# One transformer-like stack on one core: the same operations in another order of issue

## The chip, the core and the metric

The kernel runs on one core of a Trainium2 chip. The time is the device time of one execution in microseconds, and a run's figure is the median of several executions. The core has a matrix engine (TensorE, PE in the profile, with PEld for its weight loads), a vector engine (VectorE, DVE), an activation engine (ScalarE, ACT), a general engine (GpSimd, POOL), and SyncE (SP), whose queue issues all DMAs of this kernel.

## What is computed

The input is x of 8 x 512 x 512 (8 images of 512 rows and 512 columns), in fp32. Four sublayers follow each other, each with a layer norm before and after and a residual sum:

```
x = x + ln(attn0(ln(x)))    # scores = X^T X, softmax over rows, context = weights X^T
x = x + ln(ffn0(ln(x)))     # x times the sum of 8 matrices (512 x 512), / sqrt(8), + bias
x = x + ln(attn1(ln(x)))    # RMS norm, 8 query heads in 2 groups of keys and values, Wo, residual
x = x + ln(ffn1(ln(x)))     # silu(x Wg * gs) * (x Wu * us), times Wd, * ds; inner width 1408
```

Here `ln` subtracts the mean and divides by the root of the variance.

## The kernel before

The 8 images are worked through one after the other in the source, each as four tiles of 128 rows x 512. The functions `stage_attn0`, `stage_ffn0`, `stage_attn1` and `stage_ffn1` do not issue instructions. They hand operations to a recorder (`rec.add`), each with its engine, the buffers that it reads and writes, and a closure that issues its instructions. This gives 6333 operations: 1220 for TensorE, 2174 for VectorE, 1238 for ScalarE, 952 for GpSimd and 749 DMAs. `rec.issue` then calls the closures in an order that is written out in the file: the text `STEPS` holds 6333 differences, and `order()` sums them into the numbers of operations:

```
n, found = -1, []
for step in STEPS.split():
    n += int(step)
    found.append(n)
```

Each engine gets its own instructions in that order and runs them in it, and waits on semaphores where one needs another engine's result. Buffers are handed out in the same order: an operation that opens a buffer takes the one that has been free longest among those of its kind (8 PSUM banks `f`, 15 tiles `row`, 33 tiles `fr` for weights and parts, 6 tiles `big`, 11 tiles `x`). So the order also decides which earlier work a new buffer waits for. In the given order the images overlap: while one image is in `stage_ffn1`, the next one is already in its attention.

The lines that the steps below name:

- L281 loads inputs and weights. L310 writes kept weight pieces to DRAM, and L321 fetches them back for the images 1 to 7. For these images most weights and rows are split in parts (L349, L357, L364 for weights; L380, L388, L397 for rows), and the products run on fp32r parts (L410 and L420, called one after the other as two groups of matmuls).
- A layer norm is L576 (statistics), L581 (aggregate), both on VectorE, L585 and L592 on GpSimd (`rstd`), and L600 on VectorE (normalize). L619 adds the result to x, on GpSimd, for the last image on VectorE.
- A softmax row is L633 (maximum, VectorE), L640 (exponential, ScalarE), L650 and L660 (VectorE).
- `stage_attn0`: L697 transposes on TensorE two tiles at a time, L725 copies the result on ScalarE. L753 computes a block of 128 rows of the symmetric score matrix; the part left of the diagonal comes by L751 as a transpose of earlier blocks, which L767 copied to the tiles `u` on ScalarE. L783 is the context product.
- `stage_ffn0`: L671 transposes, and for image 0 L828 (the mix) multiplies by the summed matrix, which L474 adds up on VectorE and GpSimd from 28 loaded tiles.
- `stage_attn1`: L1004 values (with the weight `wv`), L1043 queries, L1071 scores, L1102 transposes, L1114 copies them on ScalarE to the place where L1132 multiplies with the values, L1145 copies the result. L1177 is the last projection of image 0.
- `stage_ffn1`: L1251 and L1260 split the transposed rows, L1315 are the gate and up products, L1334 (silu, ScalarE), L1344 (product, VectorE), L1356 and L1363 (the two parts), L1373 the down product, L1399 its scale.

Of the kernel before, what the change touches and what calls it, by code (L numbers as in the profile page):

```python
# [1450 lines left out]
1 71 1 -71 75 1 -74 75 1 -6 1 15 -87 82 6 -5 -5 6 1 834 -846 -32 38 1 1 5 3 1 1 829 -902 905 1 4 1  # L1451
-7 19 -883 -10 2 45 1 5 -68 14 874 -867 -2 -35 9 -24 1 17 77 1 1 -50 2 2 872 1 -902 76 2 -47 875
-919 -6 98 833 -832 1 5 -4 5 1 -93 97 -24 850 -938 933 -824 -78 -3 82 -7 10 810 -812 3 1 -82 19
882 1 -8 1 -839 -71 -15 936 1 -824 1 812 12 -5 9 -928 13 2 73 -1 -14 -56 -15 2 926 -912 1 -34 51
-49 34 81 -1 2 -97 908 -876 893 -2 -887 -54 1 2 259 -207 61 -112 30 -15 257 1 -155 -5 1 1 -114 939
-888 -21 85 -100 926 -823 1 -73 -15 -30 15 32 216 -148 22 1 -19 1 -74 75 1 820 1 -686 -118 1 801
-22 -655 675 -923 928 -792 -11 -18 1 -93 122 -28 133 687 -680 -139 1 27 795 -794 -25 12 117 691 1
1 -824 28 1 -156 130 1 821 2 -1 -682 -6 -133 1 1 -6 68 -39 1 -23 67 -36 31 -55 66 747 -812 71 742
-775 1 -23 8 16 1 83 -107 1 796 -772 1 759 726 -1484 743 2 -660 675 -803 814 -749 -41 1 1 -25 1 57
-41 1 -16 17 795 -761 -50 1 55 742 15 -796 766 -781 65 78 -32 33 1379 -1399 -103 1 788 -694 -215  # L1460
160 1461 -1484 1 79 29 -2 1 2 -93 -15 1 92 1 -92 1 106 -12 -114 1 1 1 109 1 -79 -13 94 1 -112 1
151 -56 -67 14 56 -75 76 23 -10 48 -121 -38 122 668 -7 -671 11 -10 -97 -15 126 1 1 22 5 -19 -6 -1
8 -6 -95 102 1 1 -8 9 -8 1 -11 12 661 -654 1 1 1 1 -48 1 -60 86 -84 83 673 711 -725 15 -8 -760 131
630 8 -757 -10 115 656 10 6 -27 8 4 1 -785 128 636 9 13 1 -22 16 699 1 -693 -6 -16 23 686 -701 70
-69 -639 -5 734 -20 -78 -744 843 -43 -810 5 782 -720 -230 942 -1 5 -2 4 -666 1 713 1 1 1 -824 112
-138 868 1 -695 696 607 -1291 583 56 -22 -12 -709 769 1 638 -686 -656 31 -44 25 15 16 605 30 -646
1 6 1291 1 -1303 622 4 -610 -4 665 1 1 -50 1 21 -650 -24 8 21 -20 27 4 -15 -29 722 -677 -4 -25 707
-718 -14 733 -723 -9 733 -18 -701 703 -707 5 7 665 -676 14 691 -662 -12 2 -1 42 603 30 -692 1316
-1256 4 644 -711 712 -708 1316 -606 -681 633 -602 649 -720 75 647 -650 631 -622 -42 -37 74 -33 43
-85 674 29 19 -641 623 1 -694 36 -34 -1 60 4 -36 42 4 587 -659 69 -40 34 7 622 -619 562 -561 -47  # L1470
-26 692 -629 -34 4 675 -738 1 63 -4 34 645 1 1 -527 -212 102 -35 -4 -4 681 -636 -1 -35 4 -8 69 5
-69 65 -64 3 1 -3 74 -40 -40 10 60 -69 84 -14 3 7 619 -625 1206 -605 -53 1 -26 -587 75 63 -62 614
9 -628 -70 71 621 7 -623 -12 626 1 -690 692 9 -778 78 58 12 -7 -35 664 -107 -662 152 -48 -26 39
1216 -563 568 -1228 32 -1 522 -552 -5 1 15 31 -35 36 534 -565 -11 7 -11 5 -4 580 -534 509 26 -566
567 -571 651 -657 42 509 -550 1 67 -62 4 567 -566 58 -56 67 -10 -58 61 8 -7 -3 507 -506 13 -10 7
470 -538 72 571 -581 20 -323 1 309 -6 10 -45 -265 301 6 4 1 -10 475 -507 7 525 -488 -1 2 488 -537
12 4 522 -806 776 679 -567 -615 -4 12 38 -45 -4 81 -69 -11 507 2 -497 35 -33 1 56 465 -520 -12 66
-53 -12 67 438 -437 438 -505 73 -5 515 -527 -93 38 505 1 1 -439 539 1 -539 514 -509 -4 438 -497
573 -473 -99 1 1 31 30 536 -535 509 -508 1 -32 540 26 -40 -862 446 -40 -371 334 -8 25 477 40 -26
-540 33 98 2 -66 6 456 -522 43 477 1 -417 419 -529 50 1 489 -539 52 513 -25 -11 -476 -46 534 25 1  # L1480
2 -454 40 -45 23 40 -461 289 53 1 -53 528 12 -11 -528 1119 -554 -36 -381 392 2 -1 -471 -69 4 1 1
46 -5 6 -46 1 1 19 1 4 95 -94 -4 1 1 557 -554 1 29 16 -44 1 75 36 -95 2 -1 2 -16 1 -3 1 32 11 88
-105 84 -61 18 -45 -347 394 44 -94 1 4 -394 398 14 55 -44 -8 2 46 2 -44 484 545 -966 -494 12 519
-19 -86 4 14 4 4 14 4 -36 -23 2 61 14 4 43 62 -60 922 -964 -60 1 60 -25 50 -107 1 102 -484 520 -40
-3 47 -60 17 4 -63 2 75 -116 21 -436 532 -101 -8 -420 535 -85 44 25 36 1 -122 77 -59 43 2 -43 1 1
163 -151 -54 2 80 -22 -59 -9 7 23 2 -1 -2 63 1 52 28 -8 -14 -5 -94 81 -79 -14 84 2 -57 -16 17 24
-43 20 38 -37 432 -337 -55 97 -606 -11 1 537 14 4 4 3 -81 2 -3 62 -21 -39 56 365 -321 -18 12 331
-311 22 -616 539 22 43 -46 38 26 -628 919 -337 22 -87 392 4 -366 919 -918 -40 41 52 -594 502 -2 -1
71 4 -12 343 -301 1 -86 1 3 100 291 -1 2 -445 51 1 402 -361 1 55 282 -320 337 -319 311 -386 -705
1092 -8 4 -282 -47 -32 46 4 4 14 4 4 304 -9 8 2 -11 -372 -122 176 -583 591 -23 44 -20 321 -383 374  # L1490
-903 905 -913 600 59 -650 -8 592 -33 -25 387 -10 2 -904 -8 1 561 44 316 -919 569 -16 -547 605 -59
2 362 -345 1 1 345 -305 -605 607 1 1 349 -33 38 7 -401 395 -398 25 -23 45 -25 371 16 -56 41 -313
324 -6 1 -451 -4 56 43 -20 48 -49 23 364 -15 -322 9 -37 366 -15 5 5 6 -979 927 -14 61 -60 -922 2
621 360 -344 302 37 -1 11 -35 -7 1 -5 -18 -275 1 293 47 -1 -31 -29 -2 -4 2 66 -37 -6 -4 -293 1 1
292 10 -6 10 -33 -295 325 -6 10 -3 74 -39 -41 1 67 -58 75 -404 388 4 -62 2 -1 58 4 7 -10 -382 393
-103 96 -3 4 10 -72 1 27 -339 380 -393 387 -96 106 -33 24 6 -41 45 -397 388 -99 64 45 -432 821
-431 1 43 -32 -367 290 67 6 -362 352 5 40 -104 74 -14 15 31 -36 37 -105 63 6 63 -68 1 9 -4 5 434
-365 -68 1 56 4 1 -4 11 -460 461 3 -10 -4 15 -10 77 -220 214 -75 -58 432 -289 -7 5 -113 5 40 -4
-148 142 -62 73 -40 36 -6 1 -437 805 1 -394 102 -5 -2 3 -509 503 -103 406 743 -1133 -4 -6 40 1 1
-154 513 -406 48 -32 -4 -11 5 -4 405 1 -391 59 -533 567 -97 5 -4 -428 421 42 -41 1 72 1 6 -69 70  # L1500
-502 1 1 488 -487 503 -502 430 -1 -442 505 -504 499 1078 -1072 20 -14 -11 1 14 315 1 1 -389 390
-327 6 4 -515 512 4 1051 -1097 5 358 -351 -481 470 35 1 10 -34 -7 11 -10 358 -316 -1 -46 -470 1
831 2 -316 -32 -4 360 -371 1104 1 -1057 -78 31 363 -359 -537 548 -570 645 1 -75 -5 1 359 734 -1100
12 359 -280 9 992 -1078 -13 1 11 1080 -1032 26 1 1 270 -258 271 -5 -261 267 -283 278 -8 -268 -77
346 -268 1 -78 39 1 1038 -992 1 992 -726 5 -279 280 715 11 -997 1 -29 1020 -726 -263 1 -38 1 -14 2
-1 2 302 -300 1 46 -37 24 1006 -1029 24 -33 34 12 266 -311 -607 906 -1 -218 -46 1004 1 -1030 3 -2
303 -300 1 1 31 -45 1 45 -31 1 31 1 263 2 -249 -62 1 14 52 1 -21 16 255 -270 -32 53 256 -276 1 2 1
289 -291 27 -14 40 244 -232 -51 1 -12 16 1 1 -17 1 1 16 246 -245 -14 1 14 67 -39 14 230 -289 262
-244 15 -32 267 -5 1 5 -4 5 1 -17 1 1 10 22 -14 1 1 -244 225 15 -250 269 -9 -5 6 -25 56 -36 1 2 34
1 -267 224 -226 -26 958 -644 -55 76 1 -334 38 -26 301 22 -334 1 334 1 -334 47 -803 1067 1 -276 -14  # L1510
313 -298 299 -326 24 12 215 -2 78 -104 34 -208 -14 3 290 -327 302 -22 -25 -6 -252 946 -942 302 1 1
23 1 -48 25 24 -73 1 1 73 -50 49 613 -684 73 -26 1 1 -259 -48 37 244 -22 23 -271 1 271 1 1 23 1 23
1 -47 -298 13 259 1 1 -272 -1 3 318 -319 320 1 -49 50 -49 50 -289 263 -275 13 308 1 -321 273 -284
81 231 -26 1 653 -627 -314 334 -278 15 -2 220 70 1 -25 -45 1 -266 45 193 -179 180 -261 44 -45 263
1 1 1 95 -267 -51 63 184 72 -71 -279 -1 256 1 -236 2 325 8 -7 8 -24 27 -26 1 -77 94 -15 -291 -43
358 -102 -177 -80 927 -593 2 -303 318 -317 318 -330 334 1 -334 298 32 7 -38 -226 2 -85 57 255 -311
-3 326 1 -326 45 266 3 35 1 -38 -289 1 36 -26 -20 33 304 -336 -2 -1 58 -40 297 1 44 10 -9 1 -59 1
1 1 11 1 -247 -27 299 -273 249 21 1 1 10 -7 9 -340 -1 8 -6 19 -11 24 -28 350 2 5 -28 -4 9 2 -319 1
330 -351 8 1 35 -1 298 -329 -1 2 -3 23 307 -306 11 1 306 -330 312 8 -316 304 1 12 -10 2 21 -309
-12 22 -34 335 -1 -10 -322 -1 325 20 -7 -14 11 -300 1 -21 -2 313 57 -40 9 36 1 -5 11 -381 382 -6  # L1520
10 -56 41 1 5 6 -373 13 364 -373 359 11 4 -62 59 -48 -14 13 -11 2 62 -11 2 -1 -352 363 -62 15 -291
# [211 lines left out]
```

## Time and profile before

| | |
|---|---|
| median of 3 runs | 1440.98 us (1439.24 to 1441.07) |
| the profiled execution | 1439.27 us |
| its span, first to last instruction | 1437.8 us |
| granted TensorE clock, mean | 0.993 of full |
| HBM read, written | 168.05 MB, 27.26 MB |

The span is what the profile's times are counted in. Busy times are the union of an engine's instructions; a matmul's end is modelled, so a busy TensorE can still hold small stalls. A line of the timeline has the start, the length, the engine, the line of the kernel, the operation, the tiles and their shapes, the count, and in brackets the engine's idle time before it with the instruction that ended it.

### The profile page before, as it was taken

The page shows a single profiled execution, that of the slowest core. Times are in us where ns is not written, and L with a number is a line of the kernel's source. Part 1 is how long each engine was busy: PE and PEld are TensorE (multiplying, and loading weights), DVE is VectorE, ACT ScalarE, POOL GpSimd, SP SyncE. Part 2 cuts the span into 40 slices and gives each one's busy share as a digit, 9 for nine tenths or more (in the row PEclk, how much of TensorE's full clock was granted, in tenths as well). Part 3 has the DMA queues.
Part 4 walks back from the last instruction along what each step waited for, and adds up shares of the span by engine and source line. Part 5 has one row for each costly group of instructions (what it writes and reads, how often), then busy time and mean ns, then how long its engine had stood idle before and what let it go on. Part 6 is the DMA issues. An engine that isn't in the chain of part 4 may idle for free.

```text
span 1437.8 us, 25008 instructions
## 1 busy us (share of the span) xinstructions
PE 1389.1 (97%) x8926; PEld 976.0 (68%) x8926; DVE 1030.0 (72%) x2175; ACT 734.4 (51%) x1638; POOL 764.5 (53%) x962
## 2 busy tenths in 40 slices
PE   6899989999999999999999999999999999999995
PEld 3445568656886668856687567865688666876784
DVE  7998886888638887388764886568874778638933
ACT  2337565682347723576335744457334583357621
POOL 6874437236851378415764177631887117850443
PEclk9999999999999999999999999999999999999998
DMA  7361287645422165124443162413624304532351
GB/s 266 130 208 57 83 264 269 201 137 191 150 92 89 38 235 176 52 74 138 165 152 107 56 210 92 169 36 134 213 81 147 118 23 165 190 121 83 117 206 47
DMA packets 123350, 197.06 MB, mean 137 GB/s; under 512 B 12496, under 2 KB 32976, under 8 KB 123216
## 3 DMA queue, kind: packets, MB, share of 16 engines
q1 hardware_dynamic: 123216, 195.36, 40.0%
q8 instruction: 73, 1.20, 0.3%
q14 instruction: 61, 0.50, 0.1%
HBM read 168.05 MB, written 27.26 MB: 136 GB/s over the span
## 4 chain that ended last, share of the span: by engine, by line
PE 76%; DVE 11%; POOL 7%; issue 3%; ACT 2%; DMA 0%; SPq 0%; POOLq 0%; DVEq 0%; ACTq 0%
PE f L1315 19%; PE f L1373 10%; PE f L410 9%; PE f L1071 8%; PE f L1132 7%; PE f L1102 5%; PE f L420 5%; PE f L753 4%; PE f L783 3%; DVE row L600 3%; POOL rstd L592 2%; POOL x L619 2%; DVE st L576 2%; PE f L1004 2%; PE f L697 1%
## 5 line engine op out<-in xcount | busy, mean ns | idle before, releaser
L1315 PE MATMUL f<-xs,fr 128*128 128x512 f32 (+1 forms) x1472 | 341.2, 383 | 1.8 <-ACT xs L1251 1.2
L1315 PEld LDWEIGHTS f<-xs,fr 128*128 128x128 f32 x1472 | 267.3, 188 | 58.2 <-issue 1.7
L633 DVE TENSOR_REDUCE s<-f 128x1 f32<-128x512 f32 x288 | 188.2, 683 | 68.2 <-PE f L1071 48.3
L640 ACT ACTIVATE row<-f,s 128x512 f32<-128x512 f32 x288 | 197.4, 696 | 57.8 <-DVE s L633 48.6
L619 POOL TENSOR_TENSOR x<-x,row 128x512 f32<-128x512 f32 x120 | 157.7, 1318 | 118.3 <-DVE row L600 96.3
L585 POOL TENSOR_SCALAR ve<-mv 128x1 f32<-128x1 f32 x224 | 60.0, 271 | 278.3 <-DVE mv L581 234.2
L1373 PE MATMUL f<-fr,hl 128*128 128x512 f32 x704 | 187.6, 396 | 0.4 <-POOL hl L1363 0.2
L410 PE MATMUL f<-fr,fr 128*128 128x512 f32 x728 | 185.0, 397 | 1.3 <-ACT big L1145 0.5
L1363 POOL TENSOR_TENSOR hl<-row,hl 128x512 fp32r<-128x512 f32 (+1 forms) x92 | 116.3, 1270 | 123.9 <-ACT hl L1356 121.8
L1114 ACT COPY big<-f 128x512 f32<-128x512 f32 x256 | 138.1, 594 | 55.8 <-PE f L1102 54.1
L1344 DVE SCALAR_TENSOR_TENSOR row<-f,us,row 128x512 f32<-128x512 f32 (+1 forms) x92 | 65.8, 720 | 136.4 <-PE f L1315 67.1
L410 PEld LDWEIGHTS f<-fr,fr 128*128 128x128 f32 x728 | 133.7, 188 | 35.4 <-ACT big L1114 1.8
L1373 PEld LDWEIGHTS f<-fr,hl 128*128 128x128 f32 x704 | 128.9, 188 | 38.8 <-issue 10.2
L660 DVE TENSOR_SCALAR row<-row,s 128x512 f32<-128x512 f32 x288 | 150.6, 549 | 1.7
L592 POOL TENSOR_TENSOR rstd<-ve,mhalf 128x1 f32<-128x1 f32 x224 | 137.6, 618 | 14.1
L1071 PE MATMUL f<-row,big 64*128 64x512 f32 x512 | 134.1, 617 | 0.0
L1356 ACT CAST hl<-row 128x512 fp32r<-128x512 f32 (+1 forms) x92 | 54.9, 603 | 144.7 <-DVE row L1344 87.7
L1132 PE MATMUL f<-big,row 128*64 128x256 f32 x1024 | 124.0, 385 | 3.5 <-ACT big L1114 3.4
L1334 ACT ACTIVATE row<-f,gs 128x512 f32<-128x512 f32 (+1 forms) x92 | 60.3, 667 | 123.4 <-PE f L1315 123.2
L388 POOL TENSOR_TENSOR fr<-big,fr 128x512 fp32r<-128x512 f32 x56 | 74.9, 1346 | 87.0 <-ACT fr L380 87.0
L397 POOL TENSOR_TENSOR fr<-fr,fr 128x512 fp32r<-128x512 f32 x84 | 110.7, 1325 | 9.7 <-ACT fr L380 3.9
L783 PE MATMUL f<-big,big 128*128 128x512 f32 x256 | 114.1, 596 | 0.0
(102 smaller groups left out, 2086.9 us busy)
## 6 DMA issues: line engine op xcount, KB each, us to landing
fr<-kept_g SPq DMA_DIRECT2D x81, 256.0 KB, 4.3
fr<-kept_u SPq DMA_DIRECT2D x81, 256.0 KB, 5.2
fr<-kept_d SPq DMA_DIRECT2D x81, 256.0 KB, 5.3
x<-in_x SPq DMA_DIRECT2D x32, 256.0 KB, 2.7
out<-x SPq DMA_DIRECT2D x32, 256.0 KB, 2.1
row<-in_factors SPq DMA_DIRECT2D x28, 256.0 KB, 4.9
row<-in_gate_t SPq DMA_DIRECT2D x11, 256.0 KB, 5.3
row<-in_up_t SPq DMA_DIRECT2D x11, 256.0 KB, 3.9
```

Source lines behind the costliest of these rows:

```text
L410: nc.tensor.matmul(both[0].t[:, :], lhs(q, k), rhs(q, k), start=(k == 0 and q == 0), stop=(k == KT - 1 and q == 1),)
L592: lambda: nc.gpsimd.tensor_tensor(rstd.t[:, :], ve.t[:, :], mhalf, ALU.pow),
L619: lambda: on.tensor_tensor(ap(xt), ap(xt), y.t[:, :], ALU.add),
L633: lambda: nc.vector.tensor_reduce(nmax.t[:, :], sc.t[:, :], AX.X, ALU.max, negate=True),
L640: lambda: nc.scalar.activation(e.t[:, :], sc.t[:, :], AF.Exp, bias=nmax.t[:, :], accum_out=tot.t[:, :]),
L660: nc.vector.tensor_scalar(e.t[:, :], e.t[:, :], rtot.t[:, :], None, ALU.mult)
L783: nc.tensor.matmul(po.t[:, :], xnT.t[:, j, ts(t, P)], wT.t[:, j, :], start=(j == 0), stop=(j == KT - 1),)
L1071: nc.tensor.matmul(scs[g].t[:, :], qT.t[gp, i, ts(s, P)], kT.t[gp, :], start=True, stop=True,)
L1114: copy(columns_of(aT)[:, :, lo : lo + DH], halves(pts[hf]))
L1132: nc.tensor.matmul(po.t[gp, : 2 * P], v.t[:, t * P + g * DH : t * P + (g + 1) * DH], columns_of(aT)[:, g * NT + t, :], start=(t == 0), sto ...
L1315: nc.tensor.matmul(bank.t[:, cut], w.t[:, ts(kt, P)], d.t[:, kt, cut], start=(n == 0), stop=(n == KT * len(xs) - 1),)
L1373: nc.tensor.matmul(pos[t].t[:, :], part.t[:, ts(t, P)], wd.t[:, :], start=(first and n == 0), stop=(last and n == len(parts) - 1),)
```

## The change

The text `STEPS` is replaced by another one of the same length. It comes from the same search for an order as the old one, which ran three times as long. The first line of each:

```
-1 71 1 -71 75 1 -74 75 1 -6 1 15 -87 82 6 -5 -5 6 1 834 -846 -32 38 1 1 5 3 1 1 829 -902 905 1 4 1
+4 86 1 -90 71 -70 71 19 1 -19 1 -72 74 8 -7 1 195 1 -195 6 8 -18 5 841 -835 1 1 -84 16 902 1 -895
```

All 6333 operations are the same, with the same instructions, tiles and buffers of each kind. What differs is their sequence on the engines and which buffer of its kind each gets. Nearly half of it is local: on TensorE 492 of 1220 operations keep their place in the engine's sequence, and half move by one place at most, nine in ten by five at most; on VectorE the figures are 441 of 2174, two and seven; on SyncE 61 of 749, five and seventeen. TensorE's sequence at the start, with the lines of the operations (image 0 up to the first L783, a comma between operations):

```
before: L697 (tiles 0, 1), L753, L751+L753, L751+L753, L751+L753, L697 (tiles 2, 3), L697, L697, ...
after:  L697 (tiles 0, 1), L753, L697 (tiles 2, 3), L751+L753, L751+L753, L751+L753, L697, L697, ...
```

ScalarE's sequence around the second and third score block of image 1 (L767 copies to `u`, L640 exponentials, L349 and L725 as above):

```
before: L725, L640, L767, L349, L640, L349, L767, L725, L349, L767, L640
after:  L640, L725, L767, L725, L767, L349, L349, L349, L349, L640, L767
```

VectorE's sequence at the end, from the first L1399 (the number is the tile of 128 rows):

```
before: L1399 1, L1399 0, L576 1, L576 0, L581 1, L1399 2, L1399 3, L576 2, L600 1, L581 2, L581 0,
        L619 1, L576 3, L600 2, L600 0, L581 3, L619 2, L619 0, L600 3, L619 3
after:  L1399 1, L1399 2, L576 1, L576 2, L1399 0, L1399 3, L581 1, L576 3, L581 2, L576 0, L600 1,
        L581 0, L581 3, L619 1, L600 2, L600 0, L619 2, L619 0, L600 3, L619 3
```

## The prediction

> **What bounds the kernel now.** I read the page's first part, then busy time by stretches, then TensorE's waits stretch by stretch, and last the timelines around the waits. The page first:
>
> ```profile
> PE 1389.1 (97%) x8926; PEld 976.0 (68%) x8926; DVE 1030.0 (72%) x2175; ACT 734.4 (51%) x1638; POOL 764.5 (53%) x962
> ```
>
> TensorE is busy 1389.1 of 1437.8 us, so a new order of the same work can take at most the other 48.7 us, and whatever stall hides inside "busy". Where the 48.7 us lie, by stretches (start:end, length, busy PE, PEld, DVE, ACT, POOL, granted clock, DMA):
>
> ```profile
> 0.00:36.00 36.00, 24.98 (x137) 14.12 (x138) 25.76 (x43) 9.98 (x21) 23.53 (x37) 0.95 0.79 266
> 36.00:96.00 60.00, 52.41 (x221) 26.59 (x220) 54.99 (x110) 19.05 (x47) 47.01 (x64) 1.00 0.49 161
> 96.00:180.00 84.00, 83.75 (x608) 47.86 (x606) 71.88 (x175) 53.10 (x126) 42.39 (x60) 1.00 0.29 90
> 180.00:216.00 36.00, 30.85 (x205) 25.10 (x204) 29.52 (x52) 23.47 (x50) 12.61 (x17) 0.95 0.82 265
> 216.00:1296.00 1080.00, 1071.85 (x6845) 767.02 (x6843) 762.00 (x1612) 563.86 (x1247) 592.83 (x728) 1.00 0.39 134
> 1296.00:1424.00 128.00, 125.26 (x917) 95.32 (x916) 79.18 (x175) 64.96 (x147) 42.38 (x53) 1.00 0.32 113
> 1424.00:1437.80 13.80, 0.00 (x0) 0.00 (x0) 6.64 (x15) 0.00 (x0) 3.80 (x7) 0.56 0.22 82
> ```
>
> Subtract busy PE from each length: 11.0 idle at the start, 7.6 in 36:96, 0.3, 5.2 in 180:216, only 8.2 in the 1080 us that follow, 2.7 before the end, 13.8 after the last matmul. Half of the idle time lies in image 0, where VectorE is the busiest engine (54.99 of 60), and the tail. The body is nearly full, and a better order has little to win there.
>
> **The change, part by part.** The counts of instructions stay the same on every engine, so the sum holds only waits that move. I decoded both orders into operations and went through the places above.
>
> Start. The first transposes (L697) need the normalized tiles 0 and 1. Before, VectorE writes them in the order 1, 0, 2, 3; after, 3, 0, 1, 2, so TensorE starts on the third and not on the second.
>
> ```profile
> 8.71 0.55 DVE L600 TENSOR_SCALAR big<-x,mv,rstd 128x512 f32<-128x512 f32 x1 [0.46 <-POOL rstd L592]
> 8.31 1.11 PE L697 MATMUL f<-ident,big 64*128 64x64 f32 x16 [8.31 <-DVE big L600]
> ```
>
> The third ends at 8.71 + 0.55 = 9.26, so the first matmul moves from 8.31 to about 9.3: +1.0. Against it, the second pair of transposes (0.55 us) moves into the wait for L767's copy ahead of the second score block (0.57 us), but the softmax rows after it end last anyway. Some of the delay is regained at the rows, as VectorE takes its statistics of image 1 earlier: I take +0.6, bounds 0 and +1.0.
>
> Image 0, 36:96. ScalarE runs its queue in order, and the copy to `u` (L767) that the third score block of image 1 needs stands behind a softmax exponential (L640) that waits 6.83 us for VectorE:
>
> ```profile
> 47.87 0.33 PE L751 MATMUL f<-ident,u 128*128 128x128 f32 x1 [3.14 <-ACT u L767]
> 55.65 0.65 PE L671 MATMUL f<-ident,row 128*128 128x128 f32 x4 [1.85 <-DVE row L600]
> ...
> 46.26 0.69 ACT L640 ACTIVATE row<-f,s 128x512 f32<-128x512 f32 x1 [6.83 <-DVE s L633]
> 46.94 0.62 ACT L349 ACTIVATE fr<-row 128x512 fp32r<-128x512 f32 x1
> 47.45 0.36 ACT L767 COPY u<-f 128x256 f32<-128x256 f32 x1
> ```
>
> After, this copy stands ahead of that exponential, and the weight split L349 at 46.94 is done at the very start. The copy can then run when its block ends (38.44 + 2.75 = 41.2), and the 3.14 us wait goes. What is late next is VectorE. The next L671 needs a row that VectorE normalizes with 34.9 us of its work queued ahead (32.7 before), the one after it 36.9 (37.6), and the last softmax row before the fourth mix 47.7 (47.2), by medians of its operations. So its queue is no shorter where TensorE meets it again. Between 0 and -3.1; I take -1.4, since VectorE has 60 - 55 = 5 us of idle time here that an earlier score block lets it use, and less than half of that is near those rows.
>
> Image 0, 180:216. Waits of 2.1, 1.3 and 1.3 us lie on the chain from the last projection (ends 180.6) through two layer norms to the gate products (193.7). VectorE's work ahead of the last normalization is 160.1 us in both orders; one statistics operation moves up by 2.5 us, and one load of `wv` moves behind the last projection. It is issued from 180.7 and takes a median 5.0 us, which lands at 185.7, ahead of its matmuls at 186.5: hidden, and up to +1.0 if the queue is longer. I take 0, bounds -1.5 and +1.0.
>
> The body, 216:1296. Who keeps TensorE waiting there:
>
> ```profile
> PE f L1132 <- ACT big L1114: 2.7, 8, 0.7
> PE f L697 <- DVE row L600: 2.3, 7, 0.5
> ```
>
> L1132 needs ScalarE's copies (L1114) of the transposes L1102. I added up the TensorE work between the last such transposes and each L1132, with the trace's start-to-start times: less than 1.5 us stands there in 14 of the 64 cases before, in 9 of 64 after. In that proportion 2.7 becomes 1.7: -1.0. Bounds: -8.2 (all idle gone) and +6.8 (the second rival).
>
> Changes of array shape. A run of matmuls that follows one of another kind costs a little more; it counts as busy and not as idle:
>
> ```profile
> 1056.56 2.10 PE L410 MATMUL f<-fr,fr 128*128 128x512 f32 x8
> 1058.49 1.09 PE L420 MATMUL f<-fr,fr 128*128 128x512 f32 x4
> ...
> 764.98 3.64 PE f L410 x16
> ```
>
> Eight alone take 1058.49 - 1056.56 = 1.93 us to the next start; sixteen in a row take 3.64, so eight take 1.82: about 0.1 us for a change. The old order has 371 changes, the new 365: -0.6. The page "Trainium Kernel Development and Optimization", Performance Expectations, calls matmul busy time a bad measure of closeness to the limit and LDWEIGHTS busy a good one; here they are 97% and 68%. By that rule more could be won than the 48.7 us, but at 0.1 us a change the 371 hold only 37 us, and the new order removes six.
>
> The tail. From the last matmul's end (1423.2) VectorE works through four layer norms, with two waits for GpSimd:
>
> ```profile
> 1427.37 1.17 DVE L600 TENSOR_SCALAR row<-row,mv,rstd 128x512 f32<-128x512 f32 x2 [0.33 <-POOL rstd L592]
> 1430.26 0.55 DVE L600 TENSOR_SCALAR row<-row,mv,rstd 128x512 f32<-128x512 f32 x1 [0.46 <-POOL rstd L592]
> ```
>
> After, all four statistics and aggregates stand ahead of the second normalization, so GpSimd has the last `rstd` early. The last sum still ends with the last matmul, and the first is free five matmuls before it in both orders. Both waits go: -0.33 - 0.46 = -0.8; at worst 0.
>
> Sum: +0.6 - 1.4 + 0 - 1.0 - 0.6 - 0.8 = -3.2 us. The profiled execution took 1439.27 us (span 1437.8), 1.7 below the median of the runs, 1440.98. So 1436.1 on its basis and 1437.8 as the median.
>
> **The clock.** The granted clock is 0.95 in 0:36 and in 180:216, where TensorE idles in pieces, and 1.00 elsewhere up to the end. One score block at reduced clock, starting at 26.41, lasts 5.22 us; the same block lasts 3.63 at 301.85. One such stretch more or less is 1.6 us, and lies inside the range. "TensorE: Matmul & The Clock Gate", Part 1, says that the window which decides this runs free of the program, so that the same kernel meets it differently from run to run. By that rule the change could gain or lose such a stretch by chance.
>
> **Rivals.** No change that can be told (within 0.2%, 2.9 us, about what a measurement of this kernel can tell from no change). The wait in 36:96 goes, but VectorE, 92% busy there, ends at the same time; then the sum is +0.6 - 0.6 - 0.8 and the body as it was: -0.8, 1440.2. For it: VectorE's queue ahead of its rows is equal or longer. Against it: the ScalarE row above shows a pure matter of order.
>
> Slower, by ScalarE's queue in attention. The 256 copies L1114 each have an operation directly ahead of them; it is one from another stage (neither a copy, an exponential nor L1145) 19 times before and 30 after. ScalarE's rows for such operations are near 0.62 us. If all 11 more are met by TensorE, 11 x 0.62 = +6.8; with the start at +1.0, the tail and the shape changes as above and no gain in 36:96, that is 1440.98 + 6.8 + 1.0 - 1.4 = 1447.4. It decides from about 5 of the 11 on (5 x 0.62 = 3.1). Against it: ScalarE is busy only 564 of 1080 us there, and most L1132 still have over 1.5 us of cover.
>
> Faster by much: all 3.1 in 36:96, half of the body's 8.2, 1.5 in 180:216, tail and changes as in the sum, nothing lost at the start: -3.1 - 4.1 - 1.5 - 0.8 - 0.6 = -10.1, 1430.9.
>
> That the table does not do what it says is not open: same operations, another sequence.
>
> **How the numbers follow.** The forecast, with its own range of 1434 to 1440, 0.36; the much faster case 0.10; no change 0.32; the slower one 0.22. Some of the forecast's part lies above -2.9 us, and a little of the even one below it, so: faster by over 0.2% 0.43, within 0.35, slower 0.22. The range leaves out half of the very fast case and less than half of the slow one: 1432 to 1446.
>
> **What would show it.** In the new profile: the first L697 at about 9.3 us; no wait of L751 for L767 near 45 us; fewer waits of L1132 for L1114 than 8 in the body; no wait for `rstd` among the last four L600; busy PE lower by half a microsecond or so. It is wrong if TensorE's idle time in the body rises above 10 us, if a wait for a DMA appears before L1004 or L1315, or if the first score block of a later image comes later than before although image 0 ended sooner.

## The result: slower by 0.4%, and the profile after

The new order takes 1445.88 us in the median of five executions (1443.36 to 1448.16), the old one 1440.87 beside it: ratio 1.0040, 95% interval 1.0029 to 1.0051. I had forecast 1437.8, and the result lies inside my range of 1432 to 1446, almost at its upper end, and on the side that I held least likely. The profiled execution took 1448.16 us, with a span of 1445.6, 7.8 more than the span before. It is the slowest of the five, and the one profiled before (1439.27) lay below its median, so the two profiles stand further apart than the medians do (5.0 us).

The first line of the page's first part:

```profile
PE 1395.1 (97%) x8926; PEld 983.1 (68%) x8926; DVE 1042.3 (72%) x2175; ACT 733.9 (51%) x1638; POOL 761.6 (53%) x962
```

And busy time in the same stretches as before, the last one to the new end (start:end, length, then busy PE, PEld, DVE, ACT, POOL, then granted clock and DMA):

```profile
0.00:36.00 36.00, 22.62 (x125) 13.01 (x126) 23.79 (x41) 10.11 (x21) 22.56 (x37) 0.91 0.66 234
36.00:96.00 60.00, 53.72 (x220) 27.63 (x219) 55.74 (x101) 18.02 (x44) 43.92 (x56) 0.97 0.62 193
96.00:180.00 84.00, 83.69 (x608) 48.21 (x607) 73.14 (x173) 53.08 (x128) 41.61 (x56) 1.00 0.22 71
180.00:216.00 36.00, 31.43 (x194) 23.92 (x193) 29.53 (x59) 22.86 (x50) 16.89 (x26) 0.91 0.81 253
216.00:1296.00 1080.00, 1070.90 (x6841) 769.01 (x6840) 766.62 (x1610) 563.48 (x1246) 591.79 (x728) 1.00 0.40 135
1296.00:1424.00 128.00, 124.68 (x912) 94.98 (x911) 83.12 (x174) 65.43 (x150) 38.45 (x49) 0.99 0.35 117
1424.00:1445.60 21.60, 8.01 (x36) 6.30 (x34) 10.34 (x21) 0.95 (x2) 6.41 (x10) 0.76 0.18 65
```

Read first the pair that one tends to skip: the number of matmuls is the same (8926), and yet TensorE is busy 6.0 us longer (1395.1 against 1389.1). The other parts of the 7.8 us are smaller. The last matmul ends at 1432.01 instead of 1423.16, so the idle time before it is 1432.01 - 1395.05 = 36.96 us against 34.06 (+2.9), and what follows it is 13.6 us against 14.7 (-1.1). So +6.0 + 2.9 - 1.1 = +7.8. In idle time alone, length less busy PE, the stretches changed by +2.4, -1.3, +0.1, -0.6, +0.9 and +1.4 (from 1296 to the last matmul): waits moved about, as forecast, and their sum is the smaller part of the loss.

Why the same matmuls take longer stands in the column ahead of DMA. The granted clock is 0.91 in 0:36, 0.97 in 36:96 and 0.91 in 180:216; before it was 0.95, 1.00 and 0.95. Cut to the places where it changes, the profile after shows pairs like these, a stretch at full clock and the one that follows it:

```profile
25.45:28.86 3.41, 0.46 (x8) 0.33 (x8) 3.41 (x6) 1.52 (x4) 3.33 (x4) 1.00 0.76 256
28.86:35.69 6.83, 6.42 (x30) 3.54 (x31) 6.83 (x7) 1.07 (x2) 5.51 (x4) 0.50 0.23 67
...
1213.29:1216.70 3.41, 1.87 (x26) 1.39 (x27) 2.82 (x6) 1.67 (x4) 1.53 (x3) 1.00 0.98 360
1216.70:1220.12 3.42, 3.42 (x5) 1.33 (x4) 2.58 (x5) 1.70 (x2) 0.00 (x0) 0.50 0.03 10
```

The clock is granted in windows of 3.41 us. A window in which TensorE is busy for only 0.46 or 1.87 us is followed by one, or two, at clock 0.50. What this does to the work is in TensorE's timeline: a context product L783 of eight matmuls, behind a wait of 2.16 us, takes 5.40 us where 3.70 is its length at full clock (the second fence, from the profile before):

```profile
1214.54 0.71 PE L697 MATMUL f<-ident,row 64*128 64x64 f32 x16 [2.16 <-DVE row L600]
...
1215.93 5.40 PE L783 MATMUL f<-big,big 128*128 128x512 f32 x8
```

```profile
1210.87 3.70 PE L783 MATMUL f<-big,big 128*128 128x512 f32 x8
```

Up to the last matmul the profile after has 27.3 us at half clock: from 28.86, 69.82, 189.29, 680.81, 1216.70 and 1363.48, two of them two windows long. The profile before has 6.8, from 26.08 and 186.51. TensorE was busy in 25.9 us of the 27.3 and in all of the 6.8. If all of that ran at half speed, the loss is 13.0 against 3.4 us, so up to 9.6 more. That is more than the 6.0 us of busy time. The two traces tell why. The matmuls that lie mostly in these windows took 26.6 us after and 7.2 before; at the mean time of the same matmuls outside them it would be 13.7 and 4.0 (an estimate). So the windows cost 12.9 and 3.2 us, 9.7 more, and the new order saves about 3.7 us of busy time elsewhere. The whole is then +9.7 for the clock, -3.7 for the other work, +2.9 for waits before the last matmul and -1.1 behind it.

Which waits empty the windows: TensorE's waits over the whole span, in total, how often, and the longest.

```profile
PE f L697 <- DVE row L600: 10.9, 8, 3.1
...
PE f L697 <- DVE row L660: 5.3, 3, 2.9
PE f L671 <- DVE row L600: 3.9, 4, 1.6
```

Before, L697 waited for rows of L600 12 times with 2.1 us as the longest (8.5 in all); now 8 times with 3.1 as the longest. Fewer and longer waits: a wait of 2 to 3 us can starve a window of 3.41, while the seven waits of 0.5 us and less for these rows in the body before halved none. Two of the long ones:

```profile
28.98 0.69 PE L697 MATMUL f<-ident,row 64*128 64x64 f32 x8 [2.86 <-DVE row L660]
...
1362.14 0.71 PE L697 MATMUL f<-ident,row 64*128 64x64 f32 x16 [3.06 <-DVE row L600]
```

The waits of 2.9 us for L660 and of 3.1 and 2.2 us for L600 end at 28.98, 1362.14 and 1214.54; halved windows begin at 28.86, 1363.48 and 1216.70.

Two profiles alone could be chance. But the mean granted clock of every execution is known, and (1 - clock) times the span is what it loses at most. In the mean that is 16.8 us over the five executions of the new order and 11.1 over 87 of the old one: 5.7 more, where the mean times differ by 5.8 (1446.10 and 1440.32). The figures hold the end behind the last matmul, where nothing is lost; it is 1 us shorter in the new order.

### The profile page after: what moved, and what is told of

It reads as the page before. It is cut to its first block, busy times and chain, and to the rows that moved or that the text cites. A ratio compares the mean times of both kernels' runs of the same rounds, so it can differ in the third digit from the quotient of the medians.

```text
span 1445.6 us, 24985 instructions
## 1 busy us (share of the span) xinstructions
PE 1395.1 (97%) x8926; PEld 983.1 (68%) x8926; DVE 1042.3 (72%) x2175; ACT 733.9 (51%) x1638; POOL 761.6 (53%) x962
## 4 chain that ended last, share of the span: by engine, by line
PE 79%; DVE 9%; POOL 5%; issue 3%; DMA 1%; ACT 1%; SPq 0%; POOLq 0%; DVEq 0%; ACTq 0%
PE f L1315 19%; PE f L1373 10%; PE f L410 10%; PE f L1071 8%; PE f L1132 7%; PE f L420 5%; PE f L1102 5%; PE f L783 4%; PE f L753 4%; DVE row L600 2%; PE f L1004 2%; PE f L697 2%; POOL rstd L592 2%; DVE st L576 1%; DVE row L547 1%
## 5 line engine op out<-in xcount | busy, mean ns | idle before, releaser
L640 ACT ACTIVATE row<-f,s 128x512 f32<-128x512 f32 x288 | 197.2, 697 | 42.7 <-DVE s L633 29.9
L1373 PE MATMUL f<-fr,hl 128*128 128x512 f32 x704 | 185.8, 395 | 0.4 <-POOL hl L1363 0.4
L1114 ACT COPY big<-f 128x512 f32<-128x512 f32 x256 | 138.3, 592 | 55.3 <-PE f L1102 54.7
L660 DVE TENSOR_SCALAR row<-row,s 128x512 f32<-128x512 f32 x288 | 158.0, 572 | 2.2
L1373 PEld LDWEIGHTS f<-fr,hl 128*128 128x128 f32 x704 | 129.5, 188 | 38.3 <-issue 11.0
L1132 PE MATMUL f<-big,row 128*64 128x256 f32 x1024 | 124.0, 385 | 2.6 <-ACT big L1114 1.7
L783 PE MATMUL f<-big,big 128*128 128x512 f32 x256 | 115.9, 603 | 0.0
```

What stands on the lines that cost most here:

```text
L640: lambda: nc.scalar.activation(e.t[:, :], sc.t[:, :], AF.Exp, bias=nmax.t[:, :], accum_out=tot.t[:, :]),
L660: nc.vector.tensor_scalar(e.t[:, :], e.t[:, :], rtot.t[:, :], None, ALU.mult)
L783: nc.tensor.matmul(po.t[:, :], xnT.t[:, j, ts(t, P)], wT.t[:, j, :], start=(j == 0), stop=(j == KT - 1),)
L1114: copy(columns_of(aT)[:, :, lo : lo + DH], halves(pts[hf]))
L1132: nc.tensor.matmul(po.t[gp, : 2 * P], v.t[:, t * P + g * DH : t * P + (g + 1) * DH], columns_of(aT)[:, g * NT + t, :], start=(t == 0), sto ...
L1373: nc.tensor.matmul(pos[t].t[:, :], part.t[:, ts(t, P)], wd.t[:, :], start=(first and n == 0), stop=(last and n == len(parts) - 1),)
```

## Experiments

All ran five rounds beside the old order on the same chip. The old order's median in the three comparisons was 1440.57, 1440.10 and 1440.36. Where the text says "the new order" without a label, its own comparison above is meant (ratio 1.0040).

Theory: the difference is the clock; waits that are longer, or stand closer together, empty more windows. Rival: rows of VectorE and GpSimd come late for image 0, and this delays the work by itself; halved windows only go along with it. The two do not exclude each other.

### Idle matmuls in the waits of the new order (e1) and of the old one (e2)

The transposes L671 and L697 get idle matmuls ahead of them, identity by identity into the bank that the transposes then overwrite. They need no late row, so they run while TensorE would wait. Each is two instructions; eight of them, 16 instructions, took 2.05 us in e1's profile.

```
+def fill(bank, n, lo):
+    for _ in range(n if split else 0):        # split holds in the path that runs here
+        nc.tensor.matmul(bank.t[:, lo : lo + P], ident, ident, start=True, stop=True)
...
 for j, r in enumerate(srcs):
+    fill(pts[0], FILL.get(("TT", *at, j), 0), 2 * P * j)     # TT: L697, image, number, half
e1: TT(0,0,0) 18, TT(0,3,1) 10, T(0,3) 5, TT(1,4,0) 8, TT(4,3,1) 6, TT(6,7,1) 7, TT(7,6,0) 10
e2: TT(0,0,0) 18, TT(0,3,0) 4, TT(0,3,1) 2, TT(1,4,0) 8, TT(0,7,0) 4                # T: L671
```

> The new order, with dummy matmuls (ident by ident, 128 columns, overwritten by the transposes that follow) on TensorE in seven places where it waits: 18 ahead of the first transposes, and 5 to 10 in the six waits of 1.6 to 3.1 us that stand ahead of a stretch at half clock (in the profiled run at 28.9, 69.8, 189.3, 680.8, 1216.7 and 1363.5 us, 23.9 us in all). Theory 1, the clock: these waits cost twice, once as idle time and once because TensorE's clock is halved for 3.4 or 6.8 us after them. With the waits filled the halved stretches go, 23.9 us at half speed = 12 us at most, and the score block at the start runs warm, 5.2 -> 3.6 us: 1432 to 1437 median, mean clock 0.995 or more. Theory 2, late rows: the loss is the waits themselves, since a row of VectorE comes late; the clock hardly matters, and the fills change nothing but the start: 1443 to 1446.

> The old order with the same kind of dummy matmuls ahead of its first transposes (18) and in its waits near 24 and 182 us (2 to 8), which stand ahead of its only two halved stretches (26.1 and 186.5 us, 6.8 us in all). Theory 1, the clock: up to 3.4 us for the two stretches and up to 1.6 us for the first score block: 1436 to 1438, so that the gap between the two orders closes. Theory 2, late rows: 1439 to 1441, and the gap to the new order stays near 5 us.

Measured: e1 1442.33 us, ratio 1.0012 (1.0002 to 1.0021), so 3.6 of the 5 us are gone. e2 1438.73, ratio 0.9989 (0.9980 to 0.9998). More work on TensorE, and less time. Both lie between the ranges that I had set for the two theories, so neither decides. What was left at half clock before the last matmul in the profiles: 54.3 to 61.1 and 197.6 to 201.0 in e1, 48.4 to 51.8 in e2. So 3.6 us still stood between the two orders, with 10.2 against 3.4 us at half clock; the rival could still have that rest.

### Old start with new rest (e3), and new start with old rest (e4)

```
e3: order = before[:590] + [op for op in after if op not in before[:590]]
e4: order = after[:590] + [op for op in before if op not in after[:590]]
```

> A splice: the first 590 operations as in the old order (up to about 140 us, the scores of image 0), all others in the new order's sequence. In the two profiled runs the new order is 5.9 us behind at 92 us and 8.9 us behind at the end, with a low of 2.2 us at 1195 us. Theory 1 and 2 both: the loss at the start goes. If losses add up, 1445.9 - 5.9 = 1440; if the body absorbs the delay of the start (a late start lets the other engines catch up), little changes: 1443 to 1446.

> The other splice: the first 590 operations as in the new order, all others in the old order's sequence. If losses add up, 1440.9 + 5.9 = 1446.8, with the halved stretches near 29 and 70 us of the new order and the one near 186 us of the old. If the loss lies in the late places (1210 and 1360 us), 1441 to 1443.

Measured: e3 1441.79, ratio 1.0015 (1.0005 to 1.0024); e4 1444.39, ratio 1.0028 (1.0018 to 1.0038). The two losses add up to that of the whole, 1.0040. The first 590 operations, about 140 us, hold about two thirds of it. In the profiles each part brings halved windows of its own. e3 has four, two of them where the old order has its two, the others from 674.2 and 1353.5, in the new rest. e4 has four too, three of them in the new start (from 26.8, two long, and 57.5), the last from 190.6. This says where the loss sits, not why.

The clocks of all executions say more. In e3, one order all the time, the time goes with the clock: of its eleven executions the three fastest (1439.75 to 1440.31) have a mean clock of 0.992, the two slowest (1445.44 and 1445.65) 0.987 and 0.988. (In the old order, whose clock varies less, it does so only loosely.) Between the orders it is not the whole account. The time lost at most by the clock, in the mean, is 14.0 us in e3 and 13.0 in e4, against 11.1 in the old order beside them. So e3 loses 2.9 us by the clock and is 1.2 slower, and e4 loses 1.9 and is 3.8 slower. By this estimate the new start costs some 2 us that are not the clock's, which would be the rival's part, and the new rest wins nearly as much back.

### Smaller cuts into the start: the first 125 operations (e6), one row (e7)

```
e6: order = before[:125] + [op for op in after if op not in before[:125]]
e7, VectorE near 26 us: -L600 (image 1), L650, L600 (image 1), L660, ...
                        +L600 (image 1), L650, L660, L600 (image 1), ...
```

> The old order for its first 125 operations (through the first score block of image 1, which starts at 26.4 us in the old order and 31.0 in the new), the new order for all others. Theory (what the new order loses, it loses in these 30 us: the clock that comes late, and the last scaling of image 0's scores that ends at 28.9 instead of 25.3): ctx of image 0 starts near 31.5 to 32.5 us, 1441 to 1442.5. Rival (the loss lies in VectorE's and GpSimd's order between 31 and 92 us): ctx starts near 32 us but image 0's first qry no earlier than 95 us, 1444 to 1446.

> The new order with one VectorE row moved: nrm (L600) of the second image's first tile goes behind the last scaling (L660) of image 0's first four scores instead of ahead of it. Theory (the late row at 28.9 us is worth its wait, and the clock window that it empties): the 2.9 us wait of L697 for L660 falls to about 1, no halved stretch at 28.9 to 32.3, 1442 to 1444. Rival (the clock alone, halved in any case as the window before is empty of matmuls): 1445 to 1447, with a wait of the same size for the L600 that was moved.

Measured: e6 1446.17, ratio 1.0049 (1.0037 to 1.0061); e7 1445.82, ratio 1.0039 (1.0026 to 1.0052). My theory missed both; e7 lies in its rival's range. e6 does not decide: the cut made a wait that neither order has, L783 for L725, 3.9 us near 31 us. e7 is plain. The wait for L660 fell from 2.86 to 1.47 us, and the moved L600 then kept TensorE waiting 1.03 and 0.63; the windows from 28.2 to 35.0 were halved all the same. To move a late row shifts the gap inside the same window.

### The ScalarE copy that my sum counted on (e5, e11)

```
e5,  ScalarE: -L640, L349, L767      e11, also on the shared block: -VectorE L633 ... ScalarE L767
              +L767, L640, L349                                     +ScalarE L767, VectorE L633 ...
```

> The old order with one ScalarE copy moved: the L767 copy of image 1's second score block goes ahead of the L640 exp that it stands behind (46.26 us in the profile of before). It does alone what the prediction's step for 36:96 priced at -1.4 us (bounds 0 and -3.1). Theory (the copy's wait is real but VectorE's queue is equal, so most of it is given back): 1439.5 to 1440.5 against 1440.6 to 1440.9 before. Rival (the wait is on the path): 1437.5 to 1438.5. Either way no wait of L751 for L767 of 3 us near 45 us.

> The old order with the L767 copy of image 1's second score block ahead of VectorE's L633 maximum of the same block, not only ahead of the L640 exp. In the run with the copy ahead of the exp alone it still began at 46.8 us, right behind the end of L633 at 46.7, though the block was done at 41.5. Theory (the two read one PSUM tile and go in the order of issue, so the copy waited for VectorE): the copy now begins near 41.6, no wait of L751 for L767 over 1 us near 45; VectorE's rows set the rest, 1439 to 1440.5 (0 to -1.5). Rival (the whole wait was on the path, as the bound of the prediction has it): 1437 to 1438. If the copy still begins behind L633's end, the theory of the PSUM tile is wrong.

Measured: e5 1440.54, ratio 1.0005 (0.9996 to 1.0014); e11 1442.31, ratio 1.0010 (1.0001 to 1.0019): no gain, then a small loss, above the 1439 to 1440.5 that I had expected. e5's timeline shows that I had the wrong cause of the copy's wait:

```profile
46.77 0.37 ACT L767 COPY u<-f 128x256 f32<-128x256 f32 x1 [6.24 <-DVE s L633]
...
46.00 0.68 DVE L633 TENSOR_REDUCE s<-f 128x1 f32<-128x512 f32 x1
```

The block was done at 41.5, and the copy, now ahead of the exponential, still began only when VectorE's maximum of the same PSUM tile ended (46.00 + 0.68). The Trainium skill, "PSUM — Partial Sum Buffer", PSUM bank collisions raise a hardware error, says that the compiler's scheduler orders any two instructions on different engines that touch the same 32-partition quadrant of one bank, reads included. The row agrees, and e11, where the copy goes ahead of the maximum, shows it too:

```profile
40.99 0.37 ACT L767 COPY u<-f 128x256 f32<-128x256 f32 x1 [2.79 <-PE f L753]
...
54.98 1.11 PE L671 MATMUL f<-ident,row 128*128 128x128 f32 x4 [4.83 <-DVE row L600]
```

The copy begins at 40.99, and the wait of L751 is gone. L671 now waits 4.83 us for VectorE's row where it waited 1.85 before. Most of what the copy gave, VectorE took back: that L671 begins at 54.98 against 55.65, and the idle time in 36:96 is 7.0 us in e5 and 6.8 in e11, against 7.6. So of the 3.1 us, 0.6 to 0.8 reach TensorE. And the waits, in one piece now, halve the clock from 52.7 to 59.5 us. At half clock before the last matmul stand 13.7 us in e5 and 20.5 in e11, against 6.8: at half speed up to 3.4 and 6.8 us more, which is as much as was won, or more.

### More waits filled, both orders (e9, e10)

```
e9:  e1 and T(0,0) 12, TT(0,5,1) 7, TT(0,7,0) 4, TT(0,6,1) 3, first L1315: 5
e10: e2 and TT(0,5,1) 7, third score block of image 1: 12
```

> The new order with idle matmuls ahead of nearly every TensorE wait of over 0.8 us that empties a clock window: the places of the first run with them, and also those near 55, 90, 190, 194 and 197 us. Theory (the clock is the whole difference between the two orders): no halved stretch before the end or one, 1436.5 to 1439, within 1 us of the old order filled likewise. Rival (late rows of VectorE and GpSimd between 31 and 92 us cost 3 us by themselves): no halved stretch either, but 1440 to 1442, 3 us or more above the old order filled likewise.

> The old order with idle matmuls at its earlier places and also ahead of image 1's third score block near 44 us and in the transposes near 87 us. Theory (clock): no halved stretch before the end, 1436 to 1438.5 against 1438.7 with the earlier fill, as one stretch of 3.4 us at half speed (1.7 us) goes. Rival (the idle matmuls delay work that has come due): 1439 to 1440.5.

Measured: e9 1440.23, ratio 1.0000 (0.9991 to 1.0009); e10 1439.47, ratio 0.9992 (0.9983 to 1.0001). The gap of 5 us between the orders is down to 0.8, and the two intervals overlap. The profile of e9 in the stretches that had lost their clock:

```profile
0.00:36.00 36.00, 30.19 (x192) 20.73 (x193) 26.57 (x46) 11.07 (x24) 23.59 (x38) 1.00 0.73 253
36.00:96.00 60.00, 55.85 (x263) 31.11 (x262) 56.28 (x103) 18.46 (x46) 45.25 (x60) 1.00 0.57 186
...
180.00:216.00 36.00, 35.22 (x246) 28.48 (x245) 30.32 (x60) 25.50 (x54) 17.29 (x26) 1.00 0.86 265
```

The clock is 1.00 in all three. No window is halved before the last matmul, in e9 nor in e10. The order is that of the new table, with its late rows. So most of the difference goes when the halved windows go.

The late rows have a price all the same, and the profiles show it. The first product of `stage_attn1` of image 0 (keys, L993) starts at 101.66 us in the new order and at 95.75 in the old: 5.9 us behind. In e9 and e10, both at full clock, it starts at 98.83 and 94.53: 4.3 us behind still. At the last matmul e9 is 2.8 us behind (1424.6 and 1421.8), so it regains 1.5 on the way. The medians stand closer, at 0.8, but over its executions e10 also loses more by the clock, 7.1 us at most against 5.1 in e9. So some 2 to 4 us of the start are not the clock's: they are the rival's, or the cost of the idle matmuls, of which e9 has 95 and e10 55. No run here parts the two.

That idle matmuls cost something is likely. Both runs came out above the range of the theory and inside the times of its rival: e9 above 1439, though not 3 us above e10, and e10, which fills one stretch more than e2 and wins nothing by it (1439.47 against 1438.73), above 1438.5. The times of e9 lie closer together, 1440.07 to 1441.28 over eleven executions, where the old order ranged from 1438.62 to 1442.70 over 33; those of e10 do not (1437.79 to 1440.78 over eleven).

### Both at their best (e8, e12)

The old order's first 590 operations with the copy moved (e8 as e5, e12 as e11), then the new rest, with idle matmuls at the places of e2 and two of e1's (e8) or at most of e9's (e12).

> The old order's first 590 operations with the L767 copy moved as in the first run of this call, then the new order, and idle matmuls (identity by identity, results overwritten) ahead of the transposes at the start, near 25, 50, 87, 186, 670 and 1350 us, in which TensorE waits anyway. Theory (the clock and the head are what the new order loses; its body has fewer waits than the old one's): no halved stretch but in the end, 1435.5 to 1437.5, below the old order with its own fills (1438.73). Rival (the body of the new order gains nothing): 1438 to 1439.5.

> The old order's first 590 operations with the copy moved as in the run before, then the new order, with idle matmuls at all places that apply. Theory (clock): no halved stretch before the end, and the new body's full-clock matmul time (5.5 us less in the profile of the plain splice than in before), 1434.5 to 1437, below both filled orders. Rival (the body gains nothing but the phase of the clock windows): 1437 to 1439.

Measured: e8 1440.06, ratio 1.0003 (0.9995 to 1.0012); e12 1439.54, ratio 0.9996 (0.9987 to 1.0005). Neither is below the filled old order, and both are above the ranges that I had set. e8 had 6.8 us left at half clock, e12 another 6.8 at other places (from 53.6). The new rest gains nothing that shows in the time. The only version here that beats both orders, barely, is the old order with a few idle matmuls, e2.

## Why the prediction was wrong, point by point

**The step that failed is the clock.** The prediction gave it no term of its own: one stretch of 1.6 us more or less, by chance, inside the range. The profiles measured 27.3 us at half clock against 6.8; over all executions the clock takes up to 5.7 us more, and with the waits filled 4.2 of the 5 us went (5.0 to 0.8). The size of one stretch was right (5.40 - 3.70 = 1.7 us). Their number was not a matter of chance alone: in the five executions of the new order the mean granted clock was 0.987 to 0.990, in the 33 of the old one beside e9 0.990 to 0.994. I had cited the Trainium skill, "TensorE: Matmul & The Clock Gate", Part 1, on the window that runs free, and concluded that the change could only hit or miss a stretch by luck. The luck is where the window's edge falls, and it is worth some us (e3 ranged from 1439.75 to 1445.65); how many gaps are long enough to starve a window is decided by the order. The same page, under HAM oscillation, gives as the rule that TensorE must have no idle gap longer than about 3.4 us. By that rule most of the stretches above would not be there: ahead of them stand single waits of 2.16, 2.86 and 3.06 us. The measurement decides.

**The waits were the second miss.** They were to fall by 1.8 us before the last matmul and rose by 2.9; the stretch from 1296 us on, which had no term, gave 1.4 of it, with the wait of 3.06 us. By the profiles the new sum is +9.7 for the clock, +2.9 for waits, -1.1 for the tail and -3.7 for other work, where I had 0, -1.8, -0.8 and -0.6.

**Start, +0.6.** The direction was right, the place and size were not. TensorE did not start on the third normalized tile: the pair's transposes go in two halves, each as its tile comes.

```profile
8.15 0.69 PE L697 MATMUL f<-ident,big 64*128 64x64 f32 x8 [8.15 <-DVE big L600]
9.15 0.69 PE L697 MATMUL f<-ident,big 64*128 64x64 f32 x8 [0.31 <-DVE big L600]
```

What came later is a wait of 2.86 us at 28.98 for a softmax row (L660), and idle time rose by 2.4 us. By the first context product the new order was 5.4 us behind, with two halved windows on the way where the old order had one. e4, the new start alone, is 3.8 us slower, and the clock accounts for half of that at most. So this term was too small even without the clock.

**36:96, -1.4.** Idle time fell by 1.3 us, as the sum had it, and the wait of L751 near 45 us is gone. But the reading behind it fell. e5 and e11 do in the old order what this step priced: 0.6 to 0.8 us of idle time, and no gain in the time, as the clock took more. The copy stood behind VectorE's maximum, not only behind the exponential, and VectorE's rows end last either way. For this step the first rival, no change, was nearer.

**180:216, 0.** Idle time -0.6 us, inside its bounds; but two windows here ran at half clock instead of one.

**Body, -1.0.** The wait of L1132 for L1114 fell as forecast, from 2.7 us in 8 waits to 1.4 in 4 (forecast 1.7). The step left out the row next to it:

```profile
PE f L697 <- DVE row L600: 2.7, 3, 2.2
PE f L697 <- DVE row L660: 1.9, 1, 1.9
PE f L1132 <- ACT big L1114: 1.4, 4, 0.5
```

Before it was 2.3 us in 7 waits, none over 0.5. The two waits of 2.2 and 1.9 us are the ones ahead of the halved windows at 1216.70 and 680.81.

**Array shape, -0.6.** It can't be told apart in the sum of busy time, which rose. Without the clock the busy time fell by about 3.7 us (the estimate above), so the sign fits; that changes of shape made the difference is not shown. The group L1373, in which no window was halved, is busy 185.8 us instead of 187.6.

**Tail, -0.8.** Measured -1.1, though one of the two waits for `rstd` stayed:

```profile
1436.93 0.55 DVE L600 TENSOR_SCALAR row<-row,mv,rstd 128x512 f32<-128x512 f32 x1 [0.46 <-POOL rstd L592]
```

**The rivals.** The slower one named ScalarE's queue ahead of L1114. Its time, 1447.4, is near the result, but its mechanism did not happen: that wait fell. Of the three signs that I had set for "wrong", none came true: idle time in the body is 9.1 us, under the 10 that I named. They looked for waits, and the loss is in busy time. One sign for "right" did tell: busy PE was to fall by half a microsecond, and it rose by 6.0.

**Open.** How the 2 to 4 us that the new start loses at full clock divide between late rows and the idle matmuls' own cost. Where exactly in the first 140 us the new order loses most: e6 was to say it and did not. Where the 3.7 us of busy time are saved.

## What to carry to other kernels

When the same instructions in another order make an engine busy longer, look at the granted clock before any wait. Don't add up TensorE's idle time alone but list the waits by length and place, because here one wait of 2 to 3 us often cost its own length and then about 1.7 us more at half clock, while short waits that lay apart cost only themselves. A few idle matmuls that need nothing late, in a bank that is overwritten next, help to separate a clock effect from a true delay. Fill both versions alike, and compare places inside the profile as well as the totals: here the totals came within 0.8 us of each other, while the start stayed 4.3 us behind.

## What the runs showed of the hardware

How empty a window must be. I counted all 3.41 us windows from 12.5 us to shortly before the last matmul in the fourteen profiled executions, by the share in which TensorE was busy. Under 0.4, all 20 were followed by half clock; from 0.4 to 0.6, 25 of 39; from 0.6 to 0.9, 5 of 226; above that none of 5,484. The five between 0.6 and 0.9 ran at half clock themselves; of the 220 at full clock none was followed by half. So there is no need for an empty window: half-empty is enough, and a wait of about 1.5 to 2 us can do it, depending on where the window's edge falls. To come back takes more: windows at half clock with a share under 0.9 were followed by another one in 10 of 11 cases, those above in none of 39.

VectorE rows that stretch beside GpSimd. The late L660 of the start took three times its usual time (1.48 us against 0.48), and the L600 ahead of it 1.40 against 0.54, while GpSimd added up matrices (L474) without a break:

```profile
25.52 0.54 DVE L600 TENSOR_SCALAR big<-x,mv,rstd 128x512 f32<-128x512 f32 x1
...
26.12 1.40 DVE L600 TENSOR_SCALAR big<-x,mv,rstd 128x512 f32<-128x512 f32 x1
27.44 1.48 DVE L660 TENSOR_SCALAR row<-row,s 128x512 f32<-128x512 f32 x1
...
25.98 6.88 POOL L474 TENSOR_TENSOR big<-big,row 128x512 f32<-128x512 f32 x5
```

The L600 that ran before these additions took 0.54 us. The Trainium skill, "SBUF — State Buffer", Who interferes with whom, describes a pair of ports that VectorE, in its two-port modes, and GpSimd share and hold for a whole instruction, so that the later one waits; these rows agree. That it helped to starve the window at 25.45 is argued from the rows. I did not test it by itself.
